# Block attention in a perceiver kernel: products written over the gathered neighbours, sums over eight keys by additions of halves

## The chip, the cores and the metric

The kernel runs on one core of a Trainium2 chip. The metric is device time in microseconds (us) of one execution. Three runs of the kernel before gave 2375.15, 2376.91 and 2381.84 us, with a median of 2376.91. One further execution was taken with the hardware profiler; it is the source of every duration below.

The core has five engines that work at the same time, each on its own queue of instructions in order: TensorE (PE, matmuls; PEld is its loading of weights), VectorE (DVE), ScalarE (ACT), GpSimd (POOL) and SyncE (SP), which here issues the DMA transfers. They wait for each other by semaphores.

## The reference

The input `x` has 16 sequences of 64 tokens with 256 channels, 1024 rows in all. Three blocks are added to it in turn:

1. Self attention and cross attention with weights rounded to FP8. The cross attention reads a context of 1601 tokens per sequence, with 16 query heads over 8 key heads of 128 channels. Its matmuls are most of the work.
2. Block attention with ternary weights. A row is normalised and quantised, and projected to query, key and value of 16 heads of 16 channels; query and key are rotated. Attention runs inside blocks of 8 consecutive rows with a causal mask:

```
scores = jnp.einsum('bnhqd,bnhkd->bnhqk', qb, kb) * scale
scores = jnp.where(causal, jnp.finfo(scores.dtype).min, scores)
attn = jax.nn.softmax(scores, axis=-1)
ctx = jnp.einsum('bnhqk,bnhkd->bnhqd', attn, vb)
```

   An output projection, a gated feed-forward layer and two residual sums follow.
3. A gated feed-forward layer with ternary weights.

The change concerns only the two `einsum` lines: for each of 1024 rows, 16 heads and 8 keys, a dot product over 16 channels (scores), and for each row, head and channel a sum over 8 keys (values).

## The kernel before

The 1024 rows are cut into NT = 8 tiles of 128 rows, one row per partition. A tile takes about 287 us of the span. The parts of a tile (cross attention of its sequences, self attention, and the last two blocks in `last_parts`) are Python generators. A heap of steps emits them interleaved: each generator is started at a hand-set step and yields the steps to its next part, shifted by hand-set numbers (`PACE`, lines 48 to 57; `"last"` is the row for `last_parts`). `last_parts` of tile i begins 82 to 95 steps after the tile's base, with 52 steps from tile to tile, so that a tile's block attention runs beside the cross attention of the tile after the next. After that the framework orders the instructions of each engine anew, by dependencies and its own estimates of durations; it also inserts the waits. For a few instructions the code keeps its own order: `ordered("dve", ...)` (L551) ties each L564, L715, L727 and L754 behind the one before it in program order, without a wait. The block attention and L310 are not tied. So an edit of some instructions can move others.

The weights, the gathered neighbours and the products of the block attention share one pool, `wp`, of ten buffers of 128 x 1024 numbers under a single tag, handed out in turn. A buffer is used anew when the last reader of its old content has finished.

Block attention of tiles 0 to 6 (lines 1121 to 1162) goes as follows. Keys and values of the tile are written to DRAM (`kv`). `near` (L1003 to L1008) reads them back so that each row has its eight neighbours beside it: a tile of 128 x 1024 for 8 of the 16 heads, in the order key j, head h, channel d. Eight transfers fill one tile; there are two for the keys and two for the values. `product` (L1010 to L1014) multiplies a tile of neighbours by the queries or the softmax weights, broadcast, into a new tile `prod` in the order head, key, channel (L1013), and sums it (L1014): over the channels for the scores (`sc`), over the keys for the values (`cx`). All of this is on VectorE. Between the two stand the mask, maximum, exponential and division (L1139 to L1150). Then `act_quant` (L976 to L1001) quantises `cx`: maximum (L980, L981), reciprocal and scale (L983, L984, L991), rounding (L986, L987, L989); TensorE transposes the result (`tr_aq`, L997), VectorE copies it (`aq_t`, L999), and TensorE multiplies it by the output weights (`po_o`, L1168).

The last tile uses other functions, `block_scores` and `block_values`, which gather neighbours by matmul and sum with additions of halves (L1061 to L1063). The change doesn't touch them.

Other lines that the prediction names: L310 takes the rounded part off a loaded weight (`wq`, `wkv`, `wproj`) on VectorE, after the cast of L309 on ScalarE, and L379 uses both parts on TensorE (`ps_q`, `ps_kv`), whose result L389 copies on ScalarE (`qn`). L624 projects the context to keys (`ps_k`), L651 and L655 send the keys through DRAM (`kh`, `kd`) and L665 reads them back transposed (`kT`). L696 are the cross attention's score matmuls (`s`), L706 scales them (`P`), L715 keeps their running maximum, L754 subtracts it, L758 is the exponential, and L772 multiplies by the context rows (`acc`), which L617 loads. L559 and L564 form the squares of the keys and their sums.

## Time and profile before

| | |
|---|---|
| median of three runs | 2376.91 us (2375.15 to 2381.84) |
| profiled execution | 2381.09 us |
| its span, first to last instruction | 2379.3 us |
| mean granted TensorE clock | 0.996 |
| TensorE busy | 2318.1 us (97%) |
| VectorE busy | 1844.9 us (78%), 4786 instructions |
| ScalarE busy | 1670.7 us (70%) |
| GpSimd busy | 746.6 us (31%) |
| products and sums of the block attention, tiles 0 to 6 | 56 instructions, 76.4 us of VectorE |

The page gives busy time of each engine, the chain of work that ended last, and the costliest groups of instructions. In a group's line stand the source line, engine, operation, output and input with their shapes, the count, and after the bar the busy time in us with the mean duration of one instruction in ns, and then the idle time of the engine just before them with what ended it. A line of the timeline has its start in us, its duration in us, engine, line and operation; several equal instructions are drawn together with a count, and in brackets stands the idle time before and who ended it. A line of the list of waits reads: who waited for whom, in sum, how often, and the longest.

### The profile page before, as it was taken

Reading aid. Unit: us, or ns where it says so; the run is one execution under the profiler, and the core shown is the slowest. Engines: PE = TensorE matmul, PEld = TensorE weight load, DVE = VectorE, ACT = ScalarE, POOL = GpSimd, SP = SyncE. Lnnn points to the kernel's source line nnn. Section 1 sums busy time; section 2 is a strip of 40 time slices with the busy share of each in tenths; the row PEclk is TensorE's granted clock in tenths of the full one; section 3 lists DMA queues with packets and bytes.
Section 4 is the critical chain, followed back from the end, with each engine's and each line's share of the span. In section 5 each row is a group of like instructions: output and inputs, shape, how many; then the busy total and the mean of one; then the engine's idle time right before and its main releaser. Section 6 shows DMA issues by size and latency. Waiting matters only on the chain.

```text
span 2379.3 us, 40465 instructions
## 1 busy us (share of the span) xinstructions
PE 2318.1 (97%) x12501; PEld 1766.1 (74%) x12509; DVE 1844.9 (78%) x4786; ACT 1670.7 (70%) x3729; POOL 746.6 (31%) x967
## 2 busy tenths in 40 slices
PE   7999999999999999999999999999999999999997
PEld 4677777777787777777778777777777777677876
DVE  6777768878878788787887879777888777876766
ACT  6767767776776777767776777777677777676631
POOL 3323223332332333332332323334333333232200
PEclk9999999999999999999999999999999999999999
DMA  8989878777977698776887769777698776965332
GB/s 271 281 234 252 231 177 240 206 186 187 269 206 195 173 224 246 195 202 176 234 230 196 202 183 248 217 196 190 179 258 212 188 184 173 276 174 140 116 98 72
DMA packets 682094, 482.82 MB, mean 203 GB/s; under 512 B 463932, under 2 KB 591896, under 8 KB 681880
## 3 DMA queue, kind: packets, MB, share of 16 engines
q1 hardware_dynamic: 681592, 480.08, 75.4%
q8 instruction: 100, 1.64, 0.3%
q14 instruction: 114, 0.93, 0.1%
q10 hardware_dynamic: 288, 0.17, 0.0%
HBM read 268.93 MB, written 112.85 MB: 160 GB/s over the span
## 4 chain that ended last, share of the span: by engine, by line
PE 75%; DVE 9%; DMA 5%; ACT 4%; issue 3%; POOL 3%; SPq 0%; ACTq 0%; DVEq 0%; POOLq 0%
PE acc L772 23%; PE ps_k L624 22%; PE s L696 13%; PE po_x L863 2%; PE po_p L332 2%; DMA kd<-kh 2%; PE ps_q L379 2%; ACT P L706 1%; DMA kT<-kd 1%; PE tr_pc L799 1%; POOL rsx L568 1%; DVE P L754 1%; PE sc L490 1%; POOL rs L226 1%; PE po_f L1274 1%
## 5 line engine op out<-in xcount | busy, mean ns | idle before, releaser
L772 PEld LDWEIGHTS acc<-ctxN,P 128*128 128x128 f32 (+1 forms) x4160 | 713.3, 191 | 212.6 <-issue 134.9
L772 PE MATMUL acc<-ctxN,P 128*128 128x257 f32 (+5 forms) x4160 | 799.8, 338 | 5.4 <-DMA ctxN<-in_ctx_n 3.3
L624 PE MATMUL ps_k<-wkx,ctxT 128*128 128x512 f32 x1600 | 757.7, 595 | 11.6 <-DVE wkx L1331 9.4
L567 POOL TENSOR_SCALAR vx<-ss 128x4 f32<-128x4 f32 (+1 forms) x402 | 162.2, 403 | 1215.3 <-DVE ss L564 803.9
L706 ACT ACTIVATE P<-s,rsx 128x128 f32<-128x128 f32 x1536 | 441.0, 374 | 142.4 <-PE s L696 131.4
L568 POOL TENSOR_TENSOR rsx<-vx,nhalf 128x4 f32<-128x4 f32 (+1 forms) x402 | 442.6, 1101 | 32.7
L624 PEld LDWEIGHTS ps_k<-wkx,ctxT 128*128 128x128 f32 x1600 | 277.3, 191 | 208.9 <-issue 188.9
L696 PE MATMUL s<-qx,kT 128*128 128x128 f32 x3072 | 411.9, 277 | 8.2 <-ACT qn L389 4.4
L696 PEld LDWEIGHTS s<-qx,kT 128*128 128x128 f32 x3072 | 377.2, 192 | 24.8 <-ACT qn L389 6.2
L715 DVE TENSOR_TENSOR M<-P,M 128x512 f32<-128x512 f32 (+1 forms) x384 | 263.0, 685 | 167.4 <-ACT P L706 146.0
L758 ACT ACTIVATE P<-P 128x512 f32<-128x512 f32 (+1 forms) x416 | 266.6, 642 | 154.9 <-DVE P L754 153.6
L651 ACT COPY kh<-ps_k 128x1024 uint16<-128x1024 uint16 x360 | 366.8, 1019 | 8.9 <-DMA kd<-kh 8.9
L559 ACT ACTIVATE sq<-ps_k 128x512 f32<-128x512 f32 (+1 forms) x402 | 243.4, 605 | 156.2 <-PE ps_k L624 128.0
L564 DVE TENSOR_REDUCE ss<-sq 128x4 f32<-128x512 f32 (+1 forms) x402 | 272.0, 677 | 18.9 <-ACT sq L559 18.5
L754 DVE TENSOR_TENSOR P<-P,mx 128x512 f32<-128x512 f32 (+1 forms) x416 | 283.2, 681 | 0.0
L226 POOL TENSOR_TENSOR rs<-ve,nhalf 128x4 f32<-128x4 f32 (+2 forms) x112 | 114.9, 1027 | 241.4 <-DVE ve L223 218.6
L232 DVE TENSOR_SCALAR qn<-qn,mv,rs 128x128 f32<-128x128 f32 x256 | 77.2, 340 | 47.8 <-POOL rs L226 47.1
L310 DVE TENSOR_TENSOR wproj<-wproj,w_hi 128x1024 fp32r<-128x1024 f32 x60 | 73.0, 1218 | 12.9 <-ACT w_hi L309 12.2
L309 ACT CAST w_hi<-wproj 128x1024 fp32r<-128x1024 f32 x60 | 63.4, 1058 | 26.8 <-DMA wproj<-wproj 26.0
L219 DVE BATCH_NORM_STATS2 st<-qn 128x6 f32<-128x128 f32 x256 | 64.5, 270 | 18.8 <-ACT qn L389 18.8
L332 PE MATMUL po_p<-wproj,cat 128*128 128x256 f32 x272 | 67.1, 293 | 0.0
L332 PE MATMUL po_p<-w_hi,cat 128*128 128x256 f32 x240 | 65.9, 308 | 0.9 <-ACT qk L1091 0.9
(254 smaller groups left out, 2763.7 us busy)
## 6 DMA issues: line engine op xcount, KB each, us to landing
kd<-kh SPq DMA_DIRECT2D x375, 256.0 KB
ctxT<-in_ctx SPq DMA_DIRECT2D x192, 256.0 KB
ctxN<-in_ctx_n SPq DMA_DIRECT2D x384, 128.0 KB
wproj<-wproj SPq DMA_DIRECT2D x68, 512.0 KB
wq<-wq SPq DMA_DIRECT2D x32, 512.0 KB
wkv<-wkv SPq DMA_DIRECT2D x32, 512.0 KB
wqx<-wqx SPq DMA_DIRECT2D x32, 512.0 KB
near<-kv SPq DMA_DIRECT2D x224, 64.0 KB
```

The lines of the kernel that those rows point to most:

```text
L332: PE.matmul(po[:, 0:H], lhsT=cat[:, h, :], rhs=w[:, h * H : (h + 1) * H], start=h + e == 0, stop=h == 3 and e == len(ws) - 1,)
L559: A.activation(sq[:n], ps[:n], AF.Square)
L564: ordered("dve", V.reduce_sum(ss[:n], sq[:n].rearrange("p (g d) -> p g d", g=4), axis=AX.X))
L568: ordered("pool", GP.tensor_tensor(rs[:n], ve[:n], nhalf[:n, 0:4], ALU.pow))
L624: PE.matmul(ps[:n, :], lhsT=st["cxT"][c // 2][:, k, o : o + n], rhs=wkx[:, k, 512 * hh : 512 * (hh + 1)], start=k == 0, stop=k == 1,)
L651: A.copy(t, src.bitcast(U16).rearrange("p (c e) -> p e c", e=2))
L696: PE.matmul(ps[:n, g * P : (g + 1) * P], lhsT=kT[:, g, 0:n], rhs=qxs[i, hh][:, bb, 2 * g : 2 * g + 2, :].rearrange("p h s -> p (h s)"), st ...
L706: A.activation(pc[:, g * P : (g + 1) * P], ps[:, g * P : (g + 1) * P], AF.Copy, scale=rs[:, g : g + 1])
L715: ordered("dve", V.tensor_tensor(st["M"][:n], pc[:n], st["M"][:n], ALU.max))
L754: ordered("dve", V.tensor_tensor(pc[:n], pc[:n], st["mx"][:n].rearrange("p g q -> p (g q)"), ALU.add))
L758: A.activation(pc[:n], pc[:n], AF.Exp)
L772: m = PE.matmul(ps, lhsT=pc[:n, g * P : (g + 1) * P], rhs=cx[:n, o : o + w], start=g < 3 and c == 0, stop=c == NC - 1, skip_group_check=g ...
```

## The change

`product` gives way to two functions. `near_scores` writes the products over the neighbours themselves, in their own order (key, head, channel), and sums over the channels with a view of that order. `near_values` also writes the products over the neighbours, with the softmax weights read in the order key, head, and sums over the eight keys by three additions: the upper half of 1024 numbers onto the lower, then of 512, then the last two parts of 128 into `cx`. No `prod` tile is allocated.

```diff
-    def product(out, x, y, order):
-
-        t = wp.tile([P, 1024], F32, tag="w", name="prod")
-        V.tensor_tensor(t.rearrange("p (h j d) -> p h j d", h=8, j=8), x, y, ALU.mult)
-        V.reduce_sum(out, t.rearrange("p (h j d) -> p " + order, h=8, j=8), axis=AX.X)
+    def near_scores(out, x, y):
+
+        y = y.rearrange("p (j x) -> p j x", j=8)
+        V.tensor_tensor(y, x.unsqueeze(1).to_broadcast([P, 8, P]), y, ALU.mult)
+        V.reduce_sum(out, y.rearrange("p j (h d) -> p h j d", h=8), axis=AX.X)
+
+    def near_values(out, x, y):
+
+        y4 = y.rearrange("p (j h d) -> p j h d", j=8, h=8)
+        V.tensor_tensor(y4, x.rearrange("p h j -> p j h").unsqueeze(3).to_broadcast([P, 8, 8, 16]), y4, ALU.mult)
+        for n in (512, 256):
+            V.tensor_tensor(y[:, 0:n], y[:, 0:n], y[:, n : 2 * n], ALU.add)
+        V.tensor_tensor(out, y[:, 0:P], y[:, P : 2 * P], ALU.add)
...
-                product(
-                    sc[:, 8 * a : 8 * a + 8, :],
-                    r1[:, a * P : (a + 1) * P].rearrange("p (h d) -> p h d", h=8).unsqueeze(2).to_broadcast([P, 8, 8, 16]),
-                    near_k[a].rearrange("p (j h d) -> p h j d", j=8, h=8), "h j d",
-                )
+                near_scores(sc[:, 8 * a : 8 * a + 8, :], r1[:, a * P : (a + 1) * P], near_k[a])
...
-                product(
-                    cx[:, a * P : (a + 1) * P].rearrange("p (h d) -> p h d", h=8),
-                    sc[:, 8 * a : 8 * a + 8, :].unsqueeze(3).to_broadcast([P, 8, 8, 16]),
-                    near_v[a].rearrange("p (j h d) -> p h j d", j=8, h=8), "h d j",
-                )
+                near_values(cx[:, a * P : (a + 1) * P], sc[:, 8 * a : 8 * a + 8, :], near_v[a])
```

The order of instructions as the framework builds it is the same in both kernels on TensorE, ScalarE, GpSimd and SP for the work around tiles 0 to 4; on VectorE, and on all engines around tiles 5 and 6, it differs.

## The prediction

> **What bounds the kernel now.** I read the page's first and fourth parts, then the list of waits of TensorE, the groups of VectorE by form, and the timelines around the places where the changed lines run.

> ```profile
> PE 2318.1 (97%) x12501; PEld 1766.1 (74%) x12509; DVE 1844.9 (78%) x4786; ACT 1670.7 (70%) x3729; POOL 746.6 (31%) x967
> PE 75%; DVE 9%; DMA 5%; ACT 4%; issue 3%; POOL 3%; SPq 0%; ACTq 0%; DVEq 0%; POOLq 0%
> ```

> TensorE is busy for 97% of the span of 2379.3 us and carries 75% of the chain that ended last. Work taken from VectorE is worth only what it takes out of TensorE's idle time. In the timeline that idle time adds up to some 57 us, and 13 us of it lie before 50 us, before any block attention. The list of waits tells who ends the rest:

> ```profile
> PE tr_aq L997 <- DVE aq_q L989: 10.5, 3, 5.3
> PE ps_kv L379 <- DVE wkv L310: 0.7, 1, 0.7
> ```

> The three waits of the first line are 4.05 us at 2267.09 (tile 6) and 5.30 and 1.13 us in the last tile, which the change does not touch.

> **What the edited instructions cost.** The groups by form (last columns: busy us, mean ns, idle before):

> ```profile
> L1014 DVE TENSOR_REDUCE cx<-prod 128x128 f32<-128x1024 f32 x14 | 26.0, 1890 | 0.0
> L1013 DVE TENSOR_TENSOR prod<-r,near 128x1024 f32<-128x1024 f32 x14 | 17.0, 1217 | 0.0
> L1014 DVE TENSOR_REDUCE sc<-prod 128x64 f32<-128x1024 f32 x14 | 16.9, 1210 | 0.0
> L1041 DVE TENSOR_REDUCE sc<-prod 128x64 f32<-128x1024 f32 x2 | 2.4, 1216 | 0.0
> L1139 DVE TENSOR_TENSOR sc<-sc,shp 128x128 f32<-128x128 f32 x8 | 2.2, 281 | 0.0
> L1062 DVE TENSOR_TENSOR prod<-prod 128x512 f32<-128x512 f32 x1 | 0.7, 692 | 0.0
> L1063 DVE TENSOR_TENSOR cx<-prod 128x256 f32<-128x256 f32 x1 | 0.4, 427 | 0.0
> ```

> *Scores, 14 pairs.* A product and a sum stay a product and a sum. The new sum reads runs of 16 elements, 128 apart; L1041 reads such runs (256 apart) at 1216 ns, and the old product read the neighbours in just this order at 1217. I take 1.21 us, so nothing changes. Bounds: 1.21, and the 1.89 of L1014, which reads single elements 16 apart; that would add 14 x 0.68 = 9.5 us of VectorE time.

> *Values, 14 pairs.* The product keeps its 1024 elements: 1.22 us (bounds 1.22 and 1.89, by the same two rows; I take 1.22 because L1061, a product tile added to in place, has 1.224). The sum of 1.89 us becomes 0.69 + 0.43 + 0.28 = 1.40 us: 0.49 us less, 6.9 us of VectorE time in all. But each addition waits for the one before. In the last tile such a chain starts at 2342.12, 2343.38, 2344.11 and its reader at 2344.57, so the steps are 1.26, 0.73, 0.46 and, for the smallest, 0.28 + 0.03 = 0.31. One group is 2.76, both are 5.4 (the second product overlaps the end of the first group by some 0.1). The old order took 2.27 + 3.60 = 5.87, as its independent instructions overlap. A tile gains 0.4 to 0.5 us, not 1.0.

> The trace speaks on the number of instructions too: 1224 and 692 ns for 1024 and 512 elements leave 1.04 ns per element and 0.16 us per instruction. [...]

> *The ring.* 28 `prod` tiles leave the ten buffers of `wp`. Loads that waited for a product now wait for something older, and the wait of the neighbours' values for a buffer moves from their first group to the second, onto the score sum of the first, which in tile 0 is 20 us old by then. In the list of SP's waits the products and their sums stand once, with 0.3 us. Gain and loss: 0. The neighbours hold their buffers until the last addition, about 1.5 us longer; the next loads into them (L258, L301) in tiles 0 to 4 are issued 12 us or more after, and in tile 6 nothing is issued behind them for 9 us.

> **What of it lies on the path: tiles 0 to 4.** The built order of TensorE, ScalarE, GpSimd and SP is the same in both kernels up to tile 4. Only VectorE's differs: the whole quantisation chain (L981 to L989) now runs ahead of L715, L754 and L564, which come 0.9 to 1.3 us later. Tile 0:

> ```profile
> 564.85 10.59 SPq L1007 DMA_DIRECT2D near<-kv  x16
> 578.11 2.35 DVE L1013 TENSOR_TENSOR prod<-sc,near 128x1024 f32<-128x1024 f32 x2
> 584.24 1.54 PE L772 MATMUL acc<-ctxN,P 128*128 128x257 f32 x6 [1.36 <-DMA ctxN<-in_ctx_n]
> ```

> The 1.36 us belong to SP: 16 issues hold it 10.6 us and a context load comes late (likewise 1.11, 0.83 and 0.79 in tiles 1 to 3, 4.1 in all). SP's order is unchanged, so this stays. The delayed L754 feeds an exponential at 586.26 whose matmul starts at 594.79; L564 feeds a weight first used at 594.08; TensorE reads `aq_q` at 588.73 and did not wait. Cover of 5 us or more: 0 for five tiles. Without the cover each would cost 1 us.

> **Tile 5 is the one that moves.**

> ```profile
> 2022.46 0.69 DVE L564 TENSOR_REDUCE ss<-sq 128x4 f32<-128x512 f32 x1 [1.03 <-ACT sq L559]
> 2023.88 1.23 DVE L310 TENSOR_TENSOR wq<-wq,w_hi 128x1024 fp32r<-128x1024 f32 x1 [0.73 <-ACT w_hi L309]
> 2025.79 0.39 PE L379 MATMUL ps_q<-wq,xq 128*128 128x512 f32 x1
> 2027.29 3.69 DVE L1014 TENSOR_REDUCE cx<-prod 128x128 f32<-128x1024 f32 x2
> 2028.04 1.16 PE L696 MATMUL s<-qx,kT 128*128 128x128 f32 x8 [0.74 <-ACT qn L389]
> 2032.17 0.39 PE L379 MATMUL ps_kv<-wkv,xq 128*128 128x256 f32 x1 [0.70 <-DVE wkv L310]
> 2039.47 2.01 PE L772 MATMUL acc<-ctxN,P 128*128 128x257 f32 x10 [0.99 <-ACT P L758]
> ```

> Before, VectorE makes `wq` (L310) and then the value products. In the built order of the new kernel both groups and the first two instructions of the quantisation (L980, L981) stand ahead of that L310, while TensorE's `ps_q` keeps its place and is in order. After the L564 of 2022.46 the block starts at 2023.06 and ends at 2028.50; L980 takes 0.45, L981 some 0.1; L310 ends at about 2030.25. TensorE wants it at 2025.79: **a new wait of 4.5 us**, with all matmuls queued behind it.

> Four old waits stood in the same stretch: the 0.74, 0.70 and 0.99 shown and 0.27 at 2041.75, in sum 2.70. I expect them to go: ScalarE, late by a cast at 2028.04, will have finished it; `wkv` will be done by 2032.7 and is wanted only at 2034.4; `tr_aq`, the rest of `acc`, `po_p` and `po_o` now stand between the scores and the `acc` that waited. Net 4.5 - 2.7 = **+1.8 us**. The key projections move 5 to 7 us later; their keys are used 20 us or more after. SP's queue is moved too: a key written 3.5 us later (kd<-kh) and a key load that waits for a later score matmul now hold the context and key loads behind them, by up to 6 us; the first of these is read some 8 us after that.

> **Tile 6.** Between L750 at 2257.80 and `aq_q` the second group is now threaded between the L754s, one L754 more stands ahead, and the block is 0.4 shorter: by the rows `aq_q` ends at about 2267.0 again. The wait of 4.05 us stays (+-0.3).

> **Sum.** 0 + 1.8 + 0. The profiled execution took 2381.09 us (span 2379.3 and 1.8 around it), so it would take 2382.9; it stood 4.18 above the median of 2376.91, and against that median the forecast is **2378.7 us**. Under 0.3% (7.1 us), about what a measurement of this kernel can tell from no change, that is "the same".

> **Rivals.**
> 1. *Slower: the block in front of `wq` costs more and nothing comes back.* It decides from about 8 us of block (against 5.4), or if the four old waits stay. Product at 1.89: +1.35; wait 5.9. `po_o` then waits for `aq_t` by some 0.65; a repeat in tile 6, whose VectorE chain also sets a TensorE wait, adds the 1.35 again. 5.9 + 0.65 + 1.35 = +7.9, 2385. The upper end of the range adds another full wait of 5.9: 2391. For it: VectorE is tight in both stretches; against: L1053 multiplies in exactly the new order at no extra cost (128x512 in 0.69).
> 2. *Faster: the waits of tiles 5 and 6 are VectorE's and go.* The new wait of 4.5 does not arise, because `wq` is not what TensorE stands at, and 2.7 (tile 5) and 4.05 + 0.54 (tile 6) vanish: -7.3, 2369.6. Against it: the order as built, and the 0.4 us by which a block gets shorter.
> 3. *It does not do what it says:* the dependent additions overlap nothing and the block keeps 5.9: wait 5.0, +2.3; still the same.

> **Chances.** Forecast with rival 3, 0.50 (2374 to 2383); slower by over 0.3%, 0.36, as an order that changes in two full stretches has more ways to lose than to win; faster 0.14. Range 2370 to 2391.

> **What would show it.** Sums of 0.69, 0.43 and 0.28 in place of 1.89; a wait of about 4.5 us of `ps_q` for `wq` at about 2026; no wait of `ps_kv`; 4 us still at `aq_q` in tile 6; the context waits of tiles 0 to 3 unchanged. I am wrong if the stretch of 2022 to 2050 differs by more than 5 us, or if tiles 0 to 4 move at all.

## The result

The changed kernel takes 2386.12 us (median of 18 runs) against 2379.97 us of the kernel before (18 runs): a ratio of 1.0030, with a 95% interval of 1.0020 to 1.0041. That is 4.8 to 9.8 us more. One of the 18 runs of the changed kernel took 3289.38 us at a mean clock of 0.684, and the ratio is worked out without it. Zero lies outside the interval, and the centre lies on the bound of 0.3% itself. The forecast was 2378.7 us, 1.8 us above the median of the three runs before; the direction is right, the size is less than a third of the 6.2 us between the medians. The time is inside the range of 2370 to 2391, but above the 2374 to 2383 that the prediction thought likeliest. Some 3 us of the time come from the base: the forecast started from the 2376.91 us of three runs, and 18 runs give 2379.97.

The profiled execution took 2385.04 us, with a span of 2383.2 us, 3.9 us longer than before; why this pair shows less than the medians do is said further down. Each engine's busy time, from the first part of the page after:

```profile
PE 2316.5 (97%) x12509; PEld 1764.9 (74%) x12509; DVE 1842.8 (77%) x4814; ACT 1668.7 (70%) x3729; POOL 740.5 (31%) x967
```

TensorE and VectorE are both busy for some 2 us less than before (2318.1 and 1844.9), and the program is longer. So the loss isn't more work on these two engines; one looks for places where TensorE stands, and for what follows them. The edited instructions, in the groups of VectorE by form (last columns: busy us, mean ns of one, idle before):

```profile
L1019 DVE TENSOR_TENSOR near<-sc,near 128x1024 f32<-128x1024 f32 x14 | 17.1, 1220 | 0.5
L1014 DVE TENSOR_REDUCE sc<-near 128x64 f32<-128x1024 f32 x14 | 16.9, 1210 | 0.0
L1021 DVE TENSOR_TENSOR near<-near 128x512 f32<-128x512 f32 x14 | 9.7, 691 | 0.4
L1021 DVE TENSOR_TENSOR near<-near 128x256 f32<-128x256 f32 x14 | 5.9, 424 | 0.4
L1022 DVE TENSOR_TENSOR cx<-near 128x128 f32<-128x128 f32 x14 | 4.1, 292 | 0.4
```

Every price of the forecast is there: products at 1.22 us, the scores' sum at 1.21, and 0.691 + 0.424 + 0.292 = 1.41 us in place of the strided sum of 1.89. The list of TensorE's waits after:

```profile
PE tr_aq L997 <- DVE aq_q L989: 10.4, 3, 5.3
PE ps_q L379 <- DVE wq L310: 4.5, 1, 4.5
PE tr_m L721 <- DVE sg L1192: 1.7, 1, 1.7
```

The second line is the new wait, to a tenth of the forecast; the wait of `ps_kv` for `wkv` (0.7) has left the list, and the first line is unchanged (10.5 before). The third line, 0.3 before, the prediction did not have. The timeline of tile 5, VectorE and then TensorE (start, duration, then the group, and in brackets the idle time before it and who ended it):

```profile
2024.03 1.22 DVE L1019 TENSOR_TENSOR near<-sc,near 128x1024 f32<-128x1024 f32 x1
2029.29 0.29 DVE L1022 TENSOR_TENSOR cx<-near 128x128 f32<-128x128 f32 x1
2030.14 1.23 DVE L310 TENSOR_TENSOR wq<-wq,w_hi 128x1024 fp32r<-128x1024 f32 x1
```

```profile
2026.34 0.59 PE L379 MATMUL ps_q<-w_hi,xq 128*128 128x512 f32 x1
2031.43 0.50 PE L379 MATMUL ps_q<-wq,xq 128*128 128x512 f32 x1 [4.50 <-DVE wq L310]
2032.44 1.23 PE L523 MATMUL po_s<-pT,vs 64*128 64x128 f32 x8
2033.60 2.07 PE L696 MATMUL s<-qx,kT 128*128 128x128 f32 x8
2035.46 1.93 PE L624 MATMUL ps_k<-wkx,ctxT 128*128 128x512 f32 x4
```

The block of both groups runs from 2024.03 to 2029.58, ahead of the L310 that makes `wq`, and all of TensorE stands at `ps_q`. Then read the durations, not only the brackets. The eight `po_s` take 1.23 us and the eight `s` 2.07 us; before, the `s` took 1.16 (the line at 2028.04 in the prediction) and the `po_s` 0.71:

```profile
2026.58 0.71 PE L523 MATMUL po_s<-pT,vs 64*128 64x128 f32 x8
```

Behind `ps_q` no matmul shown here waits any more, and yet these matmuls lose 1.5 us. The table by stretch tells why. Its columns are the stretch, its length, the busy times of PE, its weight loads, DVE, ACT and POOL with their instructions, then the granted TensorE clock, the DMA share and GB/s. After:

```profile
2031.00:2034.00 3.00, 2.57 (x13) 1.82 (x14) 2.90 (x9) 1.45 (x2) 0.00 (x0) 0.69 1.01 314
2034.00:2036.00 2.00, 2.00 (x10) 1.76 (x10) 2.00 (x5) 0.31 (x2) 0.00 (x0) 0.61 0.00 0
2036.00:2040.00 4.00, 4.00 (x26) 3.19 (x25) 4.00 (x17) 3.48 (x11) 0.00 (x0) 1.00 0.67 106
```

Before, in the same place:

```profile
2025.00:2040.00 15.00, 12.56 (x63) 8.14 (x62) 14.87 (x30) 9.70 (x18) 1.02 (x2) 1.00 1.08 300
```

The 0.69 and 0.61 are means over stretches that hold two clocks. Read in stretches of half a us, the clock is 0.50 from 2032.1 to 2035.6 and 1.00 on both sides. So after the 4.5 us in which TensorE had nothing to do, it is granted half its clock for 3.4 us; before, the same place runs at 1.00 throughout.

The account of the loss, from the start times and waits in the two timelines. The first `ps_q` of tile 5 is 0.97 us late already (2026.34 against 2025.37). The wait brings 4.50. The slow matmuls between 2031.43 and 2035.46 take 4.03 us; before, they took 3.24 with 0.74 of waiting in it, so 2.50 of work: 1.53 more. The four old waits are gone: -2.70. Later, `tr_m` waits 1.39 us more for `sg`, `tr_pc` 0.79 for `pq`, and 0.59 of `tr_r` go. Sum 0.97 + 4.50 + 1.53 - 2.70 + 1.39 + 0.79 - 0.59 = 5.89; the `tr_aq` of tile 6 is in fact 5.84 us later (2272.93 against 2267.09). The medians lie 6.2 us apart, but that the two figures are so near is in part luck: the 0.97 turns out below to be scatter.

### The profile page after: what moved, and what is told of

It reads as the page before. It is cut to its first block, busy times and chain, and to the rows that moved or that the text cites. A ratio compares the mean times of both kernels' runs of the same rounds, so it can differ in the third digit from the quotient of the medians.

```text
span 2383.2 us, 40490 instructions
## 1 busy us (share of the span) xinstructions
PE 2316.5 (97%) x12509; PEld 1764.9 (74%) x12509; DVE 1842.8 (77%) x4814; ACT 1668.7 (70%) x3729; POOL 740.5 (31%) x967
## 4 chain that ended last, share of the span: by engine, by line
PE 37%; DVE 6%; issue 3%; DMA 2%; POOL 2%; ACT 1%; SPq 1%; POOLq 0%; DVEq 0%; ACTq 0%
PE acc L772 12%; PE ps_k L624 10%; PE s L696 6%; PE po_x L863 1%; PE po_p L332 1%; POOL rsx L568 1%; PE pgu_late L1255 1%; DMA kd<-kh 1%; DVE P L754 1%; ACT P L706 1%; PE ps_q L379 1%; POOL rs L226 1%; DMA wq<-wq 0%; PE pgu L1255 0%; PE sc L490 0%
## 5 line engine op out<-in xcount | busy, mean ns | idle before, releaser
L772 PEld LDWEIGHTS acc<-ctxN,P 128*128 128x128 f32 (+1 forms) x4160 | 713.5, 190 | 211.3 <-issue 137.0
L772 PE MATMUL acc<-ctxN,P 128*128 128x257 f32 (+5 forms) x4160 | 798.7, 338 | 4.3 <-DMA ctxN<-in_ctx_n 4.3
L567 POOL TENSOR_SCALAR vx<-ss 128x4 f32<-128x4 f32 (+1 forms) x402 | 155.2, 386 | 1229.1 <-DVE ss L564 845.1
L696 PE MATMUL s<-qx,kT 128*128 128x128 f32 x3072 | 411.7, 277 | 8.5 <-ACT qn L389 4.4
L715 DVE TENSOR_TENSOR M<-P,M 128x512 f32<-128x512 f32 (+1 forms) x384 | 263.2, 685 | 177.2 <-ACT P L706 155.8
L696 PEld LDWEIGHTS s<-qx,kT 128*128 128x128 f32 x3072 | 377.4, 192 | 25.0 <-ACT qn L389 6.1
L758 ACT ACTIVATE P<-P 128x512 f32<-128x512 f32 (+1 forms) x416 | 266.2, 640 | 159.8 <-DVE P L754 158.6
L559 ACT ACTIVATE sq<-ps_k 128x512 f32<-128x512 f32 (+1 forms) x402 | 243.3, 605 | 154.8 <-PE ps_k L624 125.2
L564 DVE TENSOR_REDUCE ss<-sq 128x4 f32<-128x512 f32 (+1 forms) x402 | 272.3, 677 | 18.6 <-ACT sq L559 18.3
L754 DVE TENSOR_TENSOR P<-P,mx 128x512 f32<-128x512 f32 (+1 forms) x416 | 283.6, 682 | 0.0
L310 DVE TENSOR_TENSOR wproj<-wproj,w_hi 128x1024 fp32r<-128x1024 f32 x60 | 73.0, 1218 | 10.1 <-ACT w_hi L309 9.9
L309 ACT CAST w_hi<-wproj 128x1024 fp32r<-128x1024 f32 x60 | 63.3, 1056 | 24.3 <-DMA wproj<-wproj 23.6
```

Of the source, the lines that this page charges most:

```text
L559: A.activation(sq[:n], ps[:n], AF.Square)
L564: ordered("dve", V.reduce_sum(ss[:n], sq[:n].rearrange("p (g d) -> p g d", g=4), axis=AX.X))
L696: PE.matmul(ps[:n, g * P : (g + 1) * P], lhsT=kT[:, g, 0:n], rhs=qxs[i, hh][:, bb, 2 * g : 2 * g + 2, :].rearrange("p h s -> p (h s)"), st ...
L715: ordered("dve", V.tensor_tensor(st["M"][:n], pc[:n], st["M"][:n], ALU.max))
L754: ordered("dve", V.tensor_tensor(pc[:n], pc[:n], st["mx"][:n].rearrange("p g q -> p (g q)"), ALU.add))
L758: A.activation(pc[:n], pc[:n], AF.Exp)
```

## The experiments

My theory after the result: the loss is one place, the value block ahead of L310 in tile 5, through the wait it causes and the slow clock behind that wait. The rivals: that writing in place costs something everywhere, that three dependent additions do, or that the slow clock has nothing to do with the wait. All ratios are to the kernel before, in runs on the same chip.

**The block behind `wq` again.** The value products of tile 5 are put behind L310 by an order alone; the instructions are those of the changed kernel.

```
-    def near_values(out, x, y):
+    def near_values(out, x, y, after=None):
...
-        V.tensor_tensor(y4, ...)
+        m = V.tensor_tensor(y4, ...)
+        if after is not None:
+            behind(m, after)
...
-        V.tensor_tensor(ws, ws.bitcast(F32), hi.bitcast(F32), ALU.subtract)
+        mark["low"] = V.tensor_tensor(ws, ws.bitcast(F32), hi.bitcast(F32), ALU.subtract)
...
-                near_values(cx[...], sc[...], near_v[a])
+                near_values(cx[...], sc[...], near_v[a], mark["low"] if i == NT - 3 else None)
```

> The changed kernel with one difference: in tile 5 the two value products are tied behind the L310 of wq (an order on VectorE, no wait). As built, the order of TensorE is then that of the kernel before but for one matmul near the end. Theory 1 (the order on VectorE makes ps_q wait 4.5 us; the idle TensorE then runs at a lower granted clock for some 4 us, 1.8 us more; what follows shifts): all of the loss goes, the time is that of before, minus up to 1.5 us for the shorter block (ratio 0.9990 to 1.0005), no wait of ps_q on wq, granted clock 1.00 from 2025 to 2040. Theory 2 (the products over the neighbours or the additions themselves cost time on all tiles: buffers held longer, VectorE's port): the loss stays, ratio 1.002 or more.

Measured: 2378.20 us against 2378.27, ratio 0.9999 (0.9989 to 1.0008). In the timeline of TensorE the wait for `wq` is gone and old waits are back:

```profile
2027.04 0.39 PE L379 MATMUL ps_q<-wq,xq 128*128 128x512 f32 x1
2027.82 0.71 PE L523 MATMUL po_s<-pT,vs 64*128 64x128 f32 x8
2029.12 1.16 PE L696 MATMUL s<-qx,kT 128*128 128x128 f32 x8 [0.59 <-ACT qn L389]
```

The `po_s` and `s` take 0.71 and 1.16 us again. The whole loss hangs on this one place; in-place products and additions everywhere else cost nothing that can be measured. The `acc` that waited 0.99 us for an exponential before waits 2.06 here, so the old waits aren't a constant either; and behind these 2.06 us the ten `acc` take 3.69 us in place of 2.01, at a mean clock of 0.57 from 2041 to 2045.

**Products in tiles of their own, with the three additions.** This takes away the writing over the neighbours and keeps the arithmetic.

```
-        y = y.rearrange("p (j x) -> p j x", j=8)
-        V.tensor_tensor(y, x.unsqueeze(1).to_broadcast([P, 8, P]), y, ALU.mult)
+        n = y.rearrange("p (j x) -> p j x", j=8)
+        y = wp.tile([P, 1024], F32, tag="w", name="prod").rearrange("p (j x) -> p j x", j=8)
+        V.tensor_tensor(y, x.unsqueeze(1).to_broadcast([P, 8, P]), n, ALU.mult)
...
-        V.tensor_tensor(y4, ..., y4, ALU.mult)
+        y = wp.tile([P, 1024], F32, tag="w", name="prod")
+        t4 = y.rearrange("p (j h d) -> p j h d", j=8, h=8)
+        V.tensor_tensor(t4, ..., y4, ALU.mult)
```

> The changed kernel, but both products go into tiles of their own from the pool, as before the change; order key, head, channel and the three additions stay. As built, TensorE, ScalarE and SP keep the order of before in tile 5. Theory 1: the additions cost nothing, ratio to before 0.9990 to 1.0005, no wait of ps_q, and the list still shows 4 us at aq_q in tile 6. Theory 2, in the form that the additions cost time: ratio 1.002 or more; in the form that holding the neighbours' buffers costs time: same as theory 1.

Measured: 2377.51 us, ratio 0.9996 (0.9985 to 1.0007). VectorE's timeline in tile 5:

```profile
2020.81 1.22 DVE L310 TENSOR_TENSOR wq<-wq,w_hi 128x1024 fp32r<-128x1024 f32 x1 [1.87 <-ACT w_hi L309]
2021.95 2.35 DVE L1022 TENSOR_TENSOR prod<-sc,near 128x1024 f32<-128x1024 f32 x2
2024.22 1.96 DVE L1024 TENSOR_TENSOR prod<-prod 128x512 f32<-128x512 f32 x4
2026.10 0.49 DVE L1025 TENSOR_TENSOR cx<-prod 128x128 f32<-128x128 f32 x2
```

`wq` is made first, the two groups are threaded into each other, and the block takes 4.6 us (2021.95 to 2026.6) in place of 5.6. The built order, not the additions, separates the two kernels. Why the order comes out differently when the products have their own tiles (what the planner weighs there) wasn't tried and stays open.

**One strided sum in place of the additions, products in place.**

```
-        for n in (512, 256):
-            V.tensor_tensor(y[:, 0:n], y[:, 0:n], y[:, n : 2 * n], ALU.add)
-        V.tensor_tensor(out, y[:, 0:P], y[:, P : 2 * P], ALU.add)
+        V.reduce_sum(out.rearrange("p (h d) -> p h d", h=8), y4.rearrange("p j h d -> p h d j"), axis=AX.X)
```

> The changed kernel with products over the neighbours, but the values' sum over the keys is one strided sum instead of three additions. As built, the order in tile 5 is that of the changed kernel (block ahead of wq). Theory 1: a sum of 1.9 us in place of 1.4 makes the two groups 6.3 us long instead of 5.6, ps_q waits 5.2 us, ratio to before 1.003 to 1.0045. Theory 2, in the form that the additions cost the time: ratio 1.000.

Measured: 2388.19 us, ratio 1.0042 (1.0029 to 1.0054). The group, the wait, and the clock in the stretch behind the wait:

```profile
L1020 DVE TENSOR_REDUCE cx<-near 128x128 f32<-128x1024 f32 x14 | 27.2, 1941 | 0.4
```

```profile
PE ps_q L379 <- DVE wq L310: 5.4, 1, 5.4
```

```profile
2032.00:2034.00 2.00, 1.95 (x5) 1.20 (x7) 1.93 (x6) 0.26 (x1) 0.00 (x0) 0.50 0.55 197
2034.00:2036.00 2.00, 2.00 (x13) 1.78 (x12) 1.35 (x4) 1.27 (x2) 0.00 (x0) 0.50 0.00 0
2036.00:2038.00 2.00, 2.00 (x7) 1.33 (x6) 2.00 (x9) 1.04 (x4) 0.00 (x0) 0.50 0.03 8
2038.00:2040.00 2.00, 2.00 (x8) 1.08 (x7) 2.00 (x9) 0.45 (x2) 0.00 (x0) 0.80 0.72 149
```

The two sums take 2 x 0.5 us longer, the wait is 0.9 longer. So in that place of the order the additions keep the wait shorter. The ratio is the highest of the forms that were run, but its interval overlaps with that of the changed kernel. Behind the wait the clock is 0.50 for 6.8 us (the 0.80 of the last row leaves 0.8 us of half clock in it).

**The scores alone, and the values alone.** In each, one half of the change is undone with the earlier `product` helper.

```
-                near_values(cx[...], sc[...], near_v[a])          (scores alone)
+                product(cx[...], sc[...], near_v[a]..., "h d j")
...
-                near_scores(sc[...], r1[...], near_k[a])          (values alone)
+                product(sc[...], r1[...], near_k[a]..., "h j d")
```

> Only the scores are changed (products written over the neighbours' keys, one sum); the values keep the earlier product and strided sum. The built order of TensorE's and SyncE's instructions is that of the kernel before. My theory (the loss comes from the value block's place ahead of L310): ratio 1.000 within 0.0015, no wait of ps_q for wq, clock 1.00 in the tile-5 stretch, the 0.7 us waits for qn and wkv there. The rival (writing in place costs something in itself, because the buffer of the neighbours is freed later): half or more of the loss, ratio 1.0015 or above.

> Only the values are changed (products in place, three additions of halves); the scores keep their own tile. The built order of TensorE and SyncE is that of the changed kernel. My theory: the whole loss, ratio 1.002 to 1.004, a wait of 4.3 to 4.7 us of ps_q for wq, and after it a granted clock of 0.5 to 0.7 for some 4 us. The rival (the scores' form takes part in it): ratio under 1.0015.

Measured: scores alone 2378.12 us against 2378.94, ratio 0.9993 (0.9983 to 1.0002); values alone 2386.95, ratio 1.0034 (1.0021 to 1.0046). The timeline of TensorE with the values alone repeats that of the full change:

```profile
2032.11 0.79 PE L379 MATMUL ps_q<-wq,xq 128*128 128x512 f32 x1 [4.50 <-DVE wq L310]
2033.68 1.23 PE L523 MATMUL po_s<-pT,vs 64*128 64x128 f32 x8
2034.84 2.07 PE L696 MATMUL s<-qx,kT 128*128 128x128 f32 x8
```

The expectation of a clock of 0.5 to 0.7 for some 4 us fell short: behind the same wait of 4.50 us half clock lasts 6.8 us here (2031.8 to 2038.6) and 3.4 in the profile of the changed kernel. From the first `ps_q` behind the wait to the first `acc` (2032.11 to 2041.34) the same matmuls take 9.23 us, there 7.75 (2031.43 to 2039.18). So the clock behind one and the same wait costs 1.5 us in one execution and 3.0 in the other.

The whole loss is the values' half. With the scores alone the first `ps_q` of tile 5 starts at 2026.48 and with the block tied behind `wq` at 2026.61, against 2025.37 before and 2026.34 after: neither of these kernels is slower, so the 0.97 us that the profile pair has at that point is scatter between executions and not a cost of the change in tiles 0 to 4.

**The clock alone.** The changed kernel with 16 extra matmuls into the bank of `ps_q`, ahead of its first matmul in tile 5. Their result is overwritten (the first matmul of `ps_q` starts a new sum), so the computation is the same.

```
-    def heads(xq, ws, eps, lw, lb, out_t, side=None):
+    def heads(xq, ws, eps, lw, lb, out_t, side=None, warm=0):
...
+        for _ in range(warm):
+            PE.matmul(ps, lhsT=xq[:, 0, :], rhs=v2(ws[0])[:, 0, :], start=True, stop=True)
...
+        q = heads(..., warm=16 if (i, p) == (NT - 1, 2) else 0)
```

> The changed kernel with 16 extra matmuls of 128x512 into ps_q's own bank just before its first matmul in tile 5 (their results are overwritten); they fill some 3.7 of the 4.5 us in which TensorE waits for wq. Nothing else moves in TensorE's order. Theory 1 with the clock: the wait shrinks to under 1 us, the granted clock stays at 1.00 after it, and the time falls 1.5 to 2 us under that of the changed kernel (ratio to before about 1.002). If the low clock after the wait has another cause, the time is that of the changed kernel (1.003).

Measured: 2381.90 us, ratio 1.0017 (1.0004 to 1.0029), while the changed kernel stands at 1.0030. TensorE's timeline:

```profile
2025.41 4.01 PE L388 MATMUL ps_q<-w_hi,xq 128*128 128x512 f32 x16
2030.50 0.50 PE L379 MATMUL ps_q<-wq,xq 128*128 128x512 f32 x1 [0.85 <-DVE wq L310]
2031.40 0.71 PE L525 MATMUL po_s<-pT,vs 64*128 64x128 f32 x8
2032.14 1.16 PE L698 MATMUL s<-qx,kT 128*128 128x128 f32 x8
```

`wq` is no earlier against the start of the block of `ps_q` (5.09 us behind it in both kernels), TensorE can do nothing useful with the time, and still `po_s` and `s` take 0.71 and 1.16 us, as before the change; the granted clock is 1.00 from 2029 to 2036. So the slow matmuls are a consequence of the idle time. The 1.53 us came back in the stretch; the wait of `tr_m` for `sg` was absent too, but a wait of 2.30 of `ps_g` for `hnT` came in:

```profile
2067.47 3.38 PE L1189 MATMUL ps_g<-wup,hnT 128*128 128x512 f32 x4 [2.30 <-DVE hnT L1184]
```

These four take 1.88 us in the changed kernel's profile; the clock behind the new wait is 0.66 from 2067 to 2072. In this execution `tr_m` starts at 2074.49, against 2074.35 in the changed kernel, so nothing of the lead is left by then. The two ratios' intervals overlap as well, so the price of the clock is read from the stretch, not from the ratios.

**Warming the waits that both kernels have.** TensorE also waits for `aq_q`, 4 us in tile 6 and 5.3 in the last tile. From here on the kernel with tiles of its own is the base. Extra transposes of the identity go into the PSUM tile of `tr_aq` ahead of the real ones, which overwrite them.

```
-    def act_quant(src, w, j, last):
+    def act_quant(src, w, j, last, warm=0):
...
         tr = tr_tile("tr_aq", BF16)
+        for _ in range(warm):
+            PE.transpose(tr[:, 0:P], identb, identb)
...
-        cT, f = yield from act_quant(cx, H, 1, last)
+        cT, f = yield from act_quant(cx, H, 1, last, {NT - 2: 32, NT - 1: 48}.get(i, 0))
```

> Products in tiles of their own with the three additions (as in the kernel with own tiles), and 32 extra transposes of the identity ahead of tr_aq of the context in tile 6, 48 in the last tile, into the same PSUM tile, whose results are overwritten; nothing else in TensorE's order changes. They lie in the waits of 3.9 and 5.3 us. If TensorE's activity sets the clock after a wait: the clock after them is 1.00 instead of 0.50, the eight po_x go from 3.6 to 1.9 us, the twelve po_f of the last tile from 4.7 to 2.8 us, and the time falls by 2 to 5 us, ratio to the kernel before 0.998 to 0.999. If the clock after these waits has another cause: it stays at 0.50 and the time is that of own tiles, ratio 0.9996, or up to 2 us more where the extra transposes outlast the wait.

Measured: 2376.55 us, ratio 0.9988 (0.9979 to 0.9997). The time is as expected, the mechanism only in part: `po_x` takes 3.30 us and the first twelve `po_f` of the last tile 4.21, not 1.9 and 2.8.

```profile
2336.72 2.84 PE L997 MATMUL tr_aq<-identb 128*128 128x128 bf16 x48
2342.18 0.28 PE L999 MATMUL tr_aq<-identb,aq_q 128*128 128x128 bf16 x2 [2.62 <-DVE aq_q L989]
2343.25 4.21 PE L1279 MATMUL po_f<-w_dn,hd_late 128*128 128x256 f32 x12
```

Behind the rest of 2.62 us of idle time the clock fell all the same (0.69 and 0.50 in the next two stretches of 2 us).

**More of them.** 64 and 84 transposes in place of 32 and 48.

```
-        cT, f = yield from act_quant(cx, H, 1, last, {NT - 2: 32, NT - 1: 48}.get(i, 0))
+        cT, f = yield from act_quant(cx, H, 1, last, {NT - 2: 64, NT - 1: 84}.get(i, 0))
```

> As the kernel with 32 and 48 extra transposes, with 64 and 84. Per transpose 0.059 us (48 took 2.84), so 3.8 and 5.0 us: the waits of 3.94 and 5.30 us are nearly filled. If it was the 2.09 and 2.62 us of idle time left there that still lowered the clock to 0.73 and 0.66: now 1.00, po_x from 3.3 to 1.9 us, the last tile's first po_f from 4.2 to 2.8 us, some 3 us less than with 32 and 48, ratio to the kernel before 0.997 to 0.998. If the transposes do not count as activity (small matmuls with a weight load each): the clock after them stays at 0.5 to 0.75, and the ratio at 0.999 or above.

Measured: 2377.15 us, ratio 0.9991 (0.9981 to 1.0000): not the 0.997 to 0.998 of the expectation. In the last tile the clock stayed at 1.00 and the `po_f` took 2.76 us; in tile 6 it did harm:

```profile
2255.71 3.74 PE L997 MATMUL tr_aq<-identb 128*128 128x128 bf16 x64
2259.28 7.20 PE L772 MATMUL acc<-ctxN,P 128*128 128x257 f32 x40
2267.75 0.29 PE L999 MATMUL tr_aq<-identb,aq_q 128*128 128x128 bf16 x2 [1.26 <-DVE aq_q L989]
```

The transposes don't stand in the wait but ahead of forty `acc` matmuls that come before it. They push these back by 3.6 us (2255.71 to 2259.28), while the wait for `aq_q` shortens only from 3.94 us, with own tiles alone, to 1.26: 0.9 us lost. With 32 transposes it was 1.8 us against 1.85, nothing either way. And the clock behind it fell all the same (0.72 from 2267 to 2273), although the waits there are only 1.26 us and, for `po_o`, 0.57.

**Only the last tile.**

```
-        cT, f = yield from act_quant(cx, H, 1, last, {NT - 2: 64, NT - 1: 84}.get(i, 0))
+        cT, f = yield from act_quant(cx, H, 1, last, 84 if last else 0)
```

> As the kernel with 64 and 84 extra transposes, without the 64 in tile 6, which stood in TensorE's order ahead of the forty acc matmuls and so delayed them by 3.7 us instead of filling the wait behind them. My theory: the last tile's po_f take 2.76 and 2.76 us instead of 4.72 and 4.31 (3.5 us), the transposes outlast nothing (0.6 us of wait is left); so 2.5 to 3.5 us less than own tiles alone, ratio to the kernel before 0.998 to 0.999, tile 6 as with own tiles (wait 3.9 us, clock 0.5 behind it). If the po_f only fill time that another wait sets: ratio 0.9990 to 1.000, the saved time reappears as waits of tr_hn, tr_aq and tr_xn.

Measured: 2375.30 us against 2379.60, ratio 0.9985 (0.9974 to 0.9995). In TensorE's timeline of the last tile:

```profile
2338.61 4.85 PE L997 MATMUL tr_aq<-identb 128*128 128x128 bf16 x84
2344.08 0.28 PE L999 MATMUL tr_aq<-identb,aq_q 128*128 128x128 bf16 x2 [0.61 <-DVE aq_q L989]
2344.98 2.76 PE L1279 MATMUL po_f<-w_dn,hd_late 128*128 128x256 f32 x12
2357.38 2.76 PE L1279 MATMUL po_f<-w_dn,hd_late 128*128 128x256 f32 x12
```

The first twelve `po_f` take 2.76 us, against 4.72 with own tiles alone. This version has the lowest ratio of those run, though not clear of the two before it: some 3.6 us (1 to 6) below the kernel before and, by the two ratios, some 11 below the changed one. Its gain over own tiles alone (0.9996) isn't shown by the ratios, whose intervals overlap; the 2 us are shown in the stretch.

## Why the prediction was right or wrong

*Right: the prices.* All edited instructions cost what the rows of other shapes said, to 0.01 us, and the sum of additions beats the strided sum. Three dependent additions against one strided sum also came out as argued: one sum of 1.94 us in place of three additions of 1.41 made the wait 5.42 in place of 4.50 and the time no shorter.

*Right: where.* The new wait was forecast as 4.5 us of `ps_q` for `wq` in tile 5, and it is 4.50. The four old waits there went, the waits of tile 6 stayed. The term 4.5 - 2.7 = +1.8 stands. The experiments show that this place makes the whole loss, since putting the block behind `wq` takes all of it away. The stated condition for being wrong, more than 5 us in the stretch of 2022 to 2050, is met by the shift of 5.46 us at 2035 (6.43 less 0.97), though by 2050 the vanished waits have taken part of it back. The other condition, tiles 0 to 4 moving at all, was set too sharply: executions differ by about a us there.

*Wrong: the sum of tile 5 ended with the wait.* The step "Net 4.5 - 2.7 = +1.8 us" took TensorE to go on as before once `wq` was there. It went on at half its clock for 3.4 us, 1.53 us more (3.0 in the execution with the values alone). The rows for that lay in the profile before, behind the two waits which the forecast itself quoted as 4.05 and 5.30 us:

```profile
2267.00:2273.00 6.00, 5.37 (x15) 4.14 (x16) 4.29 (x16) 2.05 (x5) 0.93 (x1) 0.50 0.29 99
2347.00:2351.00 4.00, 3.61 (x11) 2.87 (x11) 1.85 (x6) 0.00 (x0) 0.54 (x1) 0.50 0.86 295
```

A new wait of 4.5 us lies between them in length, so a price of this kind was due: the eight `po_x` behind the first of them take 3.62 us, and 1.89 in tile 0 at full clock. The mean clock of 0.996 on the page hides it.

*Wrong: what follows later was set to nothing.* The forecast moved the key projections and SP's queue and gave both enough cover. In the profile after, `tr_m` waits 1.73 us for `sg` (0.34 before) and `tr_pc` 0.79 for `pq`, less the 0.59 of `tr_r`: 1.6 us. VectorE's timeline after shows the first of them:

```profile
2072.47 1.22 DVE L310 TENSOR_TENSOR wqx<-wqx,w_hi 128x1024 fp32r<-128x1024 f32 x1 [4.34 <-ACT w_hi L309]
2073.61 0.68 DVE L1192 SCALAR_TENSOR_TENSOR sg<-sg,ps_g 128x512 f32<-128x512 f32 x1
```

VectorE stands 4.34 us at an L310 which waits for ScalarE's cast, and `sg` is queued behind it. The cover failed on VectorE's queue, which the forecast followed only up to `wq`. The values alone and the one sum repeat this wait (1.78 and 1.05 us), and where the block stands behind `wq` it is back at 0.3; but with the clock alone, where `wq` is just as late, it is absent and another wait stands nearby. So it goes with the late stretch in three profiles of four; the links in between weren't traced, and this term is argued and not shown.

*The size of the whole.* 1.8 + 1.5 + 1.6 = 4.9 us by the account without the scatter of 0.97; the medians say 6.2, with an interval of 4.8 to 9.8. The clock behind the wait, 1.5 us in one profile and 3.0 in another, may make up the rest; the runs without a profile can't show it. The profiled pair ends only 3.9 us apart because of the clock again: in the execution before, the last tile had a second slow stretch (0.66 in 2361 to 2366), in the one after it had none (1.00), behind waits of the same 1.1 us. Rival 1 named the same place, but with a dearer block; that mechanism didn't occur, and that its 2385 us lie near the 2386.12 measured is luck. Rival 2 (the waits go) and rival 3 (the block keeps 5.9 us; it took 5.6) didn't either.

## What to carry to other kernels

When a wait is added on TensorE, look in the same trace at what TensorE's clock did behind waits of that length, and add the slow stretch to the wait: here it made a wait of 4.5 us cost 6.0 in one execution and 7.5 in another. An edit that only changes where a product is written can change the built order; ask which instructions of the engine the block now stands ahead of, and follow that engine's queue past the first victim. Where a place costs too much, an order tied at that one place may bring back what an arithmetic saving can't.

## What the runs showed of the hardware

Nor does the length tell which waits near 2 us are followed by half clock. Past the first 50 us, the profiles of the kernels before and after and of the last three kernels hold eight single waits of TensorE of 1.90 to 2.30 us. The matmuls behind four of them are slow:

| wait, us | run, place | matmuls behind it, us | the same at full clock, us |
|---|---|---|---|
| 1.90 | 64 and 84 transposes, 585 | six `acc` 2.64 | 1.54 (before, 584) |
| 2.08 | 64 and 84 transposes, 110 | four `ps_k` 3.13 | 1.88 (64 and 84 transposes, 150) |
| 2.09 | 32 and 48 transposes, 2264 | eight `po_x` 3.30 | 1.89 (tile 0) |
| 2.14 | last tile only, 147 | eight `s` 1.51 | 1.16 (before, 2028) |

Behind the other four they aren't: 2.10 (64 and 84 transposes, 149: eight `s` 1.16), 2.10 (last tile only, 77: four `ps_k` 1.98, as at a clock of 1.00 in the kernel before), 2.15 (32 and 48 transposes, 2036: ten `acc` 2.01, as at 1.00 in the kernel before) and 2.17 (the same run, 146: eight `s` 1.16). What decides near 2 us isn't shown by these runs. All longer single waits of the five profiles are followed by half clock or slow matmuls: 2.54 (before, 146), 2.62, 3.93, 3.94, 4.05, 4.50, 5.30 and 5.31 us. Single shorter waits aren't, such as 1.73 (before, 77) and 1.77 (changed kernel, 1182), with 1.00 behind both, but two of them close together can: 1.13 and 0.52 us in the last tile before have half clock from 2361.8 on, the same two in the changed kernel none (1.00 from 2366 to 2372).

The clock behind transposes. With 84 transposes of 128x128 bf16 at 0.058 us each in the wait, the clock is 1.00 behind it:

```profile
2342.00:2347.00 5.00, 4.00 (x41) 3.41 (x39) 3.23 (x14) 0.00 (x0) 0.54 (x1) 1.00 0.99 340
2347.00:2351.00 4.00, 3.43 (x12) 1.73 (x11) 1.54 (x4) 0.40 (x1) 0.00 (x0) 1.00 0.47 150
```

With own tiles alone, the stretch from 2342 to 2347, right behind the wait, has 0.50. I had left open whether transposes count as activity for the clock; behind these 84 it stayed at 1.00. These runs, in which the profile lists the transposes as MATMUL, don't show whether transposes raise a low clock.
